# Sobel layers as an interleaved pipeline with 64x64 matmul pairs

## The chip, the core and the metric

The kernel runs on one core of one Trainium2 chip. The metric is the device time of one execution in microseconds (us). A core has five engines that run beside each other, each with its own queue in program order: TensorE (matmuls, PE in the profile, its weight loads PEld), VectorE (DVE), ScalarE (ACT), GpSimd (POOL) and SyncE (SP, which issues transfers). They wait for each other through semaphores. Matmuls write to PSUM, everything else here works on SBUF, both of 128 partitions.

## The reference, cut to what matters

A network of four layers on an image of 256 x 256 pixels with 32 channels. Each layer adds to `x` a function of the group-normalised `x`. Layers 1 and 2, the Sobel layers, are the same: a 3x3 mean, then two Sobel gradients, then their magnitude.

```python
x = x + _L0_conv_ref(_gn(x), ...)     # layernorm, gated projection
x = x + _L1_conv_ref(_gn(x))          # Sobel layer
x = x + _L2_conv_ref(_gn(x))          # Sobel layer
x = x + _L3_conv_ref(_gn(x), ...)     # recurrence over 256 steps

def _L1_conv_ref(x):                  # _L2_conv_ref is the same
    kx, ky = _sobel_kernels(x.shape[-1], x.dtype)
    pooled = _avg_pool3_same(x)       # 3x3 mean, fewer neighbours at the border
    grad_x = _depthwise3(pooled, kx)
    grad_y = _depthwise3(pooled, ky)
    return jnp.sqrt(grad_x * grad_x + grad_y * grad_y + EPSILON)
```

## The kernel before

The image lies in SBUF as `xa` (or `xb`), float32, `[128, 64, 256]`: a block is 4 columns of the image with 32 channels each, which makes the 128 partitions; there are `NB = 64` blocks; the 256 elements of a block run down the image. A Sobel layer reads one of the two images and writes the other.

The filter along the 256 elements is done by additions: `u` adds neighbours, `pp` is the sum of three (with 0 beyond its ends and 1.5 times `u` at them), `v` adds neighbours of `pp`, `sh` neighbours of `v` (smoothing), and `dh` is a difference of `pp`. The filter across image columns is done by matmuls, as it mixes partitions: the block itself and its two neighbours each with a 128x128 matrix from `kt`, three products for each block and gradient. The matrices for the two neighbours (`m` 0 and 2) are zero but for the partitions of the columns next to the block.

```python
NBC = 2                                   # blocks of a step: a pair

def rows_of(ch):
    xs = src[:, ch * NBC : (ch + 1) * NBC, :]
    xn = sp.tile([P, NBC, S], F32, name="xn")
    nc.scalar.activation(xn, xs, AF.Identity, scale=scale, bias=bias)
    u = sp.tile([P, NBC, S - 1], F32, name="u")
    nc.vector.tensor_add(u, xn[:, :, 0 : S - 1], xn[:, :, 1:S])
    pp = sp.tile([P, NBC, S + 2], F32, name="pp")
    nc.gpsimd.memset(pp[:, :, 0 : S + 2 : S + 1], 0.0)
    nc.gpsimd.tensor_scalar(pp[:, :, 1 : S + 1 : S - 1], u[:, :, 0 : S - 1 : S - 2], 1.5, ...)
    nc.vector.tensor_add(pp[:, :, 2:S], u[:, :, 0 : S - 2], xn[:, :, 2:S])
    v = sp.tile([P, NBC, S + 1], F32, name="v")
    nc.vector.tensor_add(v, pp[:, :, 0 : S + 1], pp[:, :, 1 : S + 2])
    sh = kp.tile([P, NBC, S], F32, name="sh")
    nc.gpsimd.tensor_add(sh, v[:, :, 0:S], v[:, :, 1 : S + 1])
    dh = kp.tile([P, NBC, S], F32, name="dh")
    nc.vector.tensor_sub(dh, pp[:, :, 0:S], pp[:, :, 2 : S + 2])
    along[ch] = (sh, dh)

def columns_of(ch):
    ...                                   # pgs: pgx and pgy, [P, 2, S] of PSUM
    for which, pg in enumerate(pgs):
        for b in range(2):
            ...                           # taps: blocks blk - 1, blk, blk + 1
            for i, (n, m) in enumerate(taps):
                nc.tensor.matmul(pg[:, b, :], lhsT=kt[:, k0 + m, :],
                                 rhs=along[n // NBC][which][:, n % NBC, :], ...)
    nc.scalar.activation(sx, pgs[0].rearrange("p b s -> p (b s)"), AF.Square)
    nc.scalar.activation(sy, pgs[1].rearrange("p b s -> p (b s)"), AF.Square)
    nc.gpsimd.tensor_add(ss, sx, sy)
    nc.scalar.activation(mag, ss, AF.Sqrt, bias=sobel_eps)
    nc.vector.tensor_add(d, s, mag)       # residual: d in dst, s in src
    nc.vector.bn_stats(stats[:, blk // 2, :], d)

nch = NB // NBC
rows_of(0)
for ch in range(nch):
    if ch + 1 < nch:
        rows_of(ch + 1)
    columns_of(ch)
return group_norm(stats, ps_n)
```

The order of this code isn't the order in the queues: a scheduler of the framework places the instructions of this part. `xn`, `u`, `pp`, `v`, `sx`, `sy`, `ss` and `mag` have two buffers, `sh` and `dh` five, each of the two PSUM tiles three.

Of the kernel before, what the change touches and what calls it, by code (L numbers as in the profile page):

```python
# [10 lines left out]
F32 = mybir.dt.float32  # L11
AF = mybir.ActivationFunctionType
ALU = mybir.AluOpType
AX = mybir.AxisListType
PSUM = bass.MemoryType.PSUM

S = 256
# [3 lines left out]
NB = T // J  # L21
P = 128
# [9 lines left out]
K_GN, K_CEN, K_AVG, K_SOBEL = 0, 1, 2, 3  # L32
# [26 lines left out]
def net_kernel(  # L59
# [20 lines left out]
    nc = tc.nc  # L80
# [16 lines left out]
    kt = cp.tile([P, NK, P], F32, name="kt")  # L97
    nc.scalar.dma_start(out=kt, in_=consts)

    def eps_tile(value, name):  # L100
        t = cp.tile([P, 1], F32, name=name)
        nc.gpsimd.memset(t, value)
        return t
# [3 lines left out]
    sobel_eps = eps_tile(SOBEL_EPS, "sobel_eps")  # L107
# [24 lines left out]
    NST = NB // 2  # L132

    def new_stats():
        return small.tile([P, NST, nc.vector.BN_STATS_DIM], F32, name="stats")

    def group_norm(stats, psum):

        mv = small.tile([P, nc.vector.BN_AGGR_DIM], F32, name="mv")
        nc.vector.bn_aggr(mv, stats)  # L140
        pm = psum.tile([P, 1], F32, name="pm", tag="pm", bufs=1)
        nc.tensor.matmul(pm, lhsT=kt[:, K_GN, :], rhs=mv[:, 0:1], start=True, stop=True)
        mean = small.tile([P, 1], F32, name="mean")
        nc.vector.tensor_copy(mean, pm)
        d = small.tile([P, 1], F32, name="d")
        nc.vector.tensor_sub(d, mv[:, 0:1], mean)
        q = small.tile([P, 1], F32, name="q")
        nc.vector.scalar_tensor_tensor(q, d, d, mv[:, 1:2], ALU.mult, ALU.add)
        pv = psum.tile([P, 1], F32, name="pv", tag="pm", bufs=1)
        nc.tensor.matmul(pv, lhsT=kt[:, K_GN, :], rhs=q, start=True, stop=True)  # L150
        std = small.tile([P, 1], F32, name="std")
        nc.scalar.activation(std, pv, AF.Sqrt, bias=gn_eps)
        scale = small.tile([P, 1], F32, name="scale")
        nc.vector.reciprocal(scale, std)
        bias = small.tile([P, 1], F32, name="bias")
        nc.vector.scalar_tensor_tensor(bias, mean, -1.0, scale, ALU.mult, ALU.mult)
        return scale, bias


    stats = new_stats()  # L160
    WL = 32
    with tc.tile_pool(name="nat", bufs=3) as natp, tc.tile_pool(
        name="ps_in", bufs=4, space=PSUM
    ) as ps_in:
        for w0 in range(0, T, WL):
# [3 lines left out]
            for b2 in range(WL // (2 * J)):  # L169
# [9 lines left out]
                blk = w0 // J + b2 * 2  # L179
                dst = xa[:, blk : blk + 2, :].rearrange("p b s -> p (b s)")  # L180
# [19 lines left out]
    with tc.tile_pool(name="ln", bufs=3) as lnp, tc.tile_pool(  # L200
        name="ps_ln", bufs=2, space=PSUM
# [7 lines left out]
        for bat in range(NBAT):  # L209
            pvar = ps_var.tile([P, KB, 2, 2, J], F32, name="pvar")  # L210
            for i in range(KB):
                k = bat * KB + i
                src = xa[:, 2 * k : 2 * k + 2, :].rearrange("p b s -> p (b s)")
                dst = xb[:, 2 * k : 2 * k + 2, :].rearrange("p b s -> p (b s)")
                pc = ps_ln.tile([P, 2 * S], F32, name="pc")
                nc.tensor.matmul(pc, lhsT=cen, rhs=src, start=True, stop=True)
                sq = lnp.tile([P, 2, 2, P], F32, name="sq")
# [4 lines left out]
                for b in range(2):  # L222
                    for h in range(2):
                        nc.tensor.matmul(
                            pvar[:, i, b, h, :],
                            lhsT=sq[:, b, h, :],
                            rhs=kt[:, K_AVG, 0:P:C],
                            start=True,
                            stop=True,
# [11 lines left out]
            for i in range(KB):  # L241
                k = bat * KB + i
                pb = ps_ln.tile([P, 2, 2, P], F32, name="pb", bufs=2)
                for b in range(2):
                    for h in range(2):
# [3 lines left out]
                            lhsT=spread[:, r * J : (r + 1) * J, :].rearrange("p j c -> p (j c)"),  # L249
                            rhs=rstdt,  # L250
                            start=True,
                            stop=True,
# [8 lines left out]
    stats = new_stats()  # L261
    with tc.tile_pool(name="at", bufs=3) as atp, tc.tile_pool(
        name="ps_g", bufs=4, space=PSUM
# [55 lines left out]
        gn = group_norm(stats, ps_gn)  # L319


    NBC = 2

    def sobel_layer(src, dst, scale, bias):
        stats = new_stats()
        with tc.tile_pool(name="sob", bufs=2) as sp, tc.tile_pool(
            name="sobk", bufs=5
        ) as kp, tc.tile_pool(name="ps_s", bufs=3, space=PSUM) as ps_s, tc.tile_pool(
            name="ps_n", bufs=1, space=PSUM
        ) as ps_n:  # L330
            along = {}

            def rows_of(ch):

                xs = src[:, ch * NBC : (ch + 1) * NBC, :]
                xn = sp.tile([P, NBC, S], F32, name="xn")
                nc.scalar.activation(xn, xs, AF.Identity, scale=scale, bias=bias)
                u = sp.tile([P, NBC, S - 1], F32, name="u")
                nc.vector.tensor_add(u, xn[:, :, 0 : S - 1], xn[:, :, 1:S])

                pp = sp.tile([P, NBC, S + 2], F32, name="pp")
                nc.gpsimd.memset(pp[:, :, 0 : S + 2 : S + 1], 0.0)  # L342
                nc.gpsimd.tensor_scalar(
                    pp[:, :, 1 : S + 1 : S - 1],
                    u[:, :, 0 : S - 1 : S - 2],
                    1.5,
                    None,
                    ALU.mult,
                )
                nc.vector.tensor_add(pp[:, :, 2:S], u[:, :, 0 : S - 2], xn[:, :, 2:S])  # L350
                v = sp.tile([P, NBC, S + 1], F32, name="v")
                nc.vector.tensor_add(v, pp[:, :, 0 : S + 1], pp[:, :, 1 : S + 2])
                sh = kp.tile([P, NBC, S], F32, name="sh")
                nc.gpsimd.tensor_add(sh, v[:, :, 0:S], v[:, :, 1 : S + 1])
                dh = kp.tile([P, NBC, S], F32, name="dh")
                nc.vector.tensor_sub(dh, pp[:, :, 0:S], pp[:, :, 2 : S + 2])
                along[ch] = (sh, dh)

            def columns_of(ch):
                for b2 in range(NBC // 2):  # L360
                    pgs = [
                        ps_s.tile([P, 2, S], F32, name="pgx"),
                        ps_s.tile([P, 2, S], F32, name="pgy"),
                    ]
                    for which, pg in enumerate(pgs):
                        for b in range(2):
                            blk = ch * NBC + b2 * 2 + b
                            k0 = K_SOBEL + 5 * which
                            mid = 3 if blk == 0 else 4 if blk == NB - 1 else 1
                            taps = [  # L370
                                (n, m)
                                for n, m in ((blk - 1, 0), (blk, mid), (blk + 1, 2))
                                if 0 <= n < NB
                            ]
                            for i, (n, m) in enumerate(taps):
                                nc.tensor.matmul(  # L376
                                    pg[:, b, :],
                                    lhsT=kt[:, k0 + m, :],
                                    rhs=along[n // NBC][which][:, n % NBC, :],
                                    start=(i == 0),  # L380
                                    stop=(i == len(taps) - 1),
                                )
                    blk = ch * NBC + b2 * 2
                    sx = sp.tile([P, 2 * S], F32, name="sx")
                    nc.scalar.activation(sx, pgs[0].rearrange("p b s -> p (b s)"), AF.Square)
                    sy = sp.tile([P, 2 * S], F32, name="sy")
                    nc.scalar.activation(sy, pgs[1].rearrange("p b s -> p (b s)"), AF.Square)  # L387
                    ss = sp.tile([P, 2 * S], F32, name="ss")
                    nc.gpsimd.tensor_add(ss, sx, sy)  # L389
                    mag = sp.tile([P, 2 * S], F32, name="mag")  # L390
                    nc.scalar.activation(mag, ss, AF.Sqrt, bias=sobel_eps)
                    d = dst[:, blk : blk + 2, :].rearrange("p b s -> p (b s)")
                    s = src[:, blk : blk + 2, :].rearrange("p b s -> p (b s)")
                    nc.vector.tensor_add(d, s, mag)
                    nc.vector.bn_stats(stats[:, blk // 2, :], d)

            nch = NB // NBC
            rows_of(0)
            for ch in range(nch):
                if ch + 1 < nch:  # L400
                    rows_of(ch + 1)
                columns_of(ch)
            return group_norm(stats, ps_n)

    gn = sobel_layer(xa, xb, *gn)
    gn = sobel_layer(xb, xa, *gn)
    second.close()

# [379 lines left out]
```

## Time and profile before

| | us |
|---|---|
| median of 3 runs | 3195.89 |
| lowest, highest | 3186.38, 3203.14 |
| profiled execution, span | 3194.4 |
| start of the first Sobel layer's `xn` | 414.8 |
| start of the second one's | 630.5 |
| end of the second, with its statistics | 845.8 |

A profile line of a group or of the order of time names the engine, the line of the kernel, the operation, and the tiles as out<-in; `L389 POOL ... ss<-sx,sy` is GpSimd's sum of the two squares. A float32 matmul of the program shows as two instructions in the trace. In the order of time the first number is the start and the second the length, both in us; what stands in brackets is how long the engine had been idle before, and what ended that. A two-input addition of VectorE that shows more than its usual 0.68 us includes a wait that its queue doesn't show.

The groups of the Sobel layers within the whole of the page: TensorE's `pgx` and `pgy` take 183.3 and 179.4 us for 760 instructions each; the engine was idle 21.6 and 41.2 us just before them.

### The profile page before, as it was taken

How to read it: one execution, taken by the hardware profiler on the slowest of the kernel's cores; microseconds unless marked ns; L12 is line 12 of the kernel's file. 1: busy time of each engine (PE TensorE's matmuls, PEld its weight loads, DVE VectorE, ACT ScalarE, POOL GpSimd, SP SyncE). 2: the span in 40 equal slices, each digit the busy share in tenths (PEclk: the TensorE clock that was granted, in tenths of full speed). 3: DMA queues.
4: the chain of work that ended last, by engine and by line, in shares of the span. 5: the costliest groups of instructions: out<-in, count | busy, mean ns of one | idle time of the engine just before them, and what ended most of it. 6: DMA issues, size and time to landing. Idle time of an engine off the chain costs nothing.

```text
span 3194.4 us, 41235 instructions
## 1 busy us (share of the span) xinstructions
PE 2968.1 (93%) x11221; PEld 1292.2 (40%) x11221; DVE 2708.6 (85%) x6576; ACT 1931.5 (60%) x5272; POOL 1743.4 (55%) x2358
## 2 busy tenths in 40 slices
PE   6999988798799999999999999999999999999998
PEld 4744466576433333333333333333333333333332
DVE  3488886686589999999999999999999999999997
ACT  3255533333266667666666666667666666666665
POOL 0200044454356666666666666666666666666665
PEclk7999999999799999999999999999999999999999
DMA  3000000000000000000000000000000000000000
GB/s 120 1 1 1 1 1 1 1 1 1 26 15 8 14 7 15 15 8 16 8 15 7 14 8 15 15 8 16 8 15 7 14 7 15 15 8 17 2 7 9
DMA packets 29946, 38.56 MB, mean 12 GB/s; under 512 B 6244, under 2 KB 22917, under 8 KB 29704
## 3 DMA queue, kind: packets, MB, share of 16 engines
q1 hardware_dynamic: 27392, 33.57, 3.7%
q10 hardware_dynamic: 2312, 2.25, 0.2%
q8 instruction: 92, 1.51, 0.2%
q14 instruction: 150, 1.23, 0.1%
HBM read 10.63 MB, written 8.39 MB: 6 GB/s over the span
## 4 chain that ended last, share of the span: by engine, by line
DVE 40%; PE 37%; POOL 12%; issue 5%; ACT 4%; DVEq 0%; POOLq 0%; DMA 0%; ACTq 0%
DVE ve L643 13%; PE zz L630 10%; POOL rs L646 9%; DVE zn L650 7%; PE zz L625 7%; DVE c L671 6%; DVE c L679 5%; PE pg L271 3%; PE pt L689 3%; POOL ss L389 2%; PE px L704 2%; PE pv L271 2%; PE zz L614 2%; DVE h L686 2%; PE pg L296 2%
## 5 line engine op out<-in xcount | busy, mean ns | idle before, releaser
L646 POOL TENSOR_TENSOR rs<-ve,mhalf 128x4 f32<-128x4 f32 x1024 | 1035.8, 1012 | 282.5 <-DVE ve L643 240.4
L630 PE MATMUL zz<-wc,hT 128*128 128x512 f32 x2040 | 962.4, 594 | 1.2 <-DVE hT L694 1.2
L666 ACT ACTIVATE ga<-zn 128x384 f32<-128x384 f32 x1024 | 531.2, 519 | 468.0 <-DVE zn L650 467.5
L650 DVE TENSOR_TENSOR zn<-zz,rs 128x512 f32<-128x512 f32 x1024 | 701.3, 685 | 84.0 <-POOL rs L646 76.7
L675 POOL TENSOR_TENSOR fc<-ga,c 128x128 f32<-128x128 f32 x1020 | 464.9, 456 | 523.7 <-ACT ga L666 523.7
L643 DVE TENSOR_REDUCE ve<-sq 128x4 f32<-128x516 f32 x1024 | 697.2, 681 | 16.5 <-POOL sq L581 14.1
L638 ACT ACTIVATE sq<-zz 128x512 f32<-128x512 f32 x1024 | 605.2, 591 | 26.7 <-PE zz L630 13.9
L614 PE MATMUL zz<-fx,xt 33*128 33x512 f32 x2048 | 584.8, 644 | 11.4 <-DVE zn L650 7.6
L625 PE MATMUL zz<-wc,hT 128*128 128x512 f32 x1024 | 525.5, 595 | 0.0
L689 PEld LDWEIGHTS pt<-ident,h 128*128 128x128 f32 x1024 | 142.1, 139 | 805.0 <-DVE h L686 714.3
L630 PEld LDWEIGHTS zz<-wc,hT 128*128 128x128 f32 x2040 | 359.9, 197 | 264.3 <-DVE hT L694 214.1
L683 ACT ACTIVATE th<-c 128x128 f32<-128x128 f32 x1024 | 311.2, 304 | 184.6 <-DVE c L679 179.9
L689 PE MATMUL pt<-ident,h 128*128 128x128 f32 x1024 | 322.1, 315 | 87.6 <-DVE h L686 79.2
L679 DVE TENSOR_TENSOR c<-c,fc 128x128 f32<-128x128 f32 x1020 | 291.4, 286 | 55.4 <-DVE c L671 1.4
L671 DVE TENSOR_TENSOR c<-ga 128x128 f32<-128x128 f32 x1024 | 303.3, 296 | 39.2 <-ACT ga L668 39.2
L668 ACT ACTIVATE ga<-zn 128x128 f32<-128x128 f32 x1024 | 303.1, 296 | 0.0
L686 DVE TENSOR_TENSOR h<-ga,th 128x128 f32<-128x128 f32 x1024 | 291.8, 285 | 0.8 <-ACT th L683 0.8
L614 PEld LDWEIGHTS zz<-fx,xt 33*128 33x128 f32 x2048 | 156.2, 185 | 297.7 <-PE zz L630 226.0
L376 PE MATMUL pgy<-dh,kt 128*128 128x256 f32 x760 | 179.4, 386 | 41.2 <-ACT sy L387 41.2
L342 POOL MEMSET pp<- 128x4 f32 x64 | 6.4, 102 | 379.2 <-PE pg L296 244.7
L376 PE MATMUL pgx<-sh,kt 128*128 128x256 f32 x760 | 183.3, 392 | 21.6 <-POOL pp L342 13.1
L282 ACT ACTIVATE sg<-pg 128x512 f32<-128x512 f32 x256 | 128.9, 627 | 109.6 <-PE pg L271 109.6
(131 smaller groups left out, 2844.0 us busy)
## 6 DMA issues: line engine op xcount, KB each, us to landing
xt<-xa SPq DMA_DIRECT2D x256, 64.0 KB, 2.0
nat<-in_x_dram SPq DMA_DIRECT2D x16, 512.0 KB, 6.5
out_dram<-st SPq DMA_DIRECT2D x32, 256.0 KB, 2.3
wc<-in_L_conv_W_cell_dram ACTq DMA_DIRECT2D x2, 512.0 KB, 4.6
kt<-in_consts_dram ACTq DMA_DIRECT2D x1, 832.0 KB
wv<-in_L_conv_Wv_dram ACTq DMA_DIRECT2D x4, 32.0 KB, 4.5
wg<-in_L_conv_Wg_dram ACTq DMA_DIRECT2D x4, 32.0 KB, 4.2
gamma<-in_L_conv_ln_gamma_dram ACTq DMA_DIRECT2D x4, 0.1 KB, 6.5
```

The source lines that it names most:

```text
L614: nc.tensor.matmul(zz, lhsT=x, rhs=fx[rows, l, :], start=True, stop=l == 0 and t == 0)
L625: nc.tensor.matmul(get("zz"), lhsT=v["hT", 0, t][:, seqs], rhs=wc[:, l, 0, :], start=False, stop=t == 0)
L630: nc.tensor.matmul(get("zz"), lhsT=v["hT", l, t - 1][:, seqs], rhs=wc[:, l, 1, :], start=False, stop=True,)
L638: nc.scalar.activation(sqs[l, h][:, :, 0:H], four(get("zz")), AF.Square, scale=float(H**-0.5))
L643: nc.vector.tensor_reduce(ve, sqs[l, h], AX.X, ALU.add)
L646: nc.gpsimd.tensor_tensor(rs, get("ve"), mhalf, ALU.pow)
L650: nc.vector.tensor_mul(four(zn), four(get("zz")), get("rs").unsqueeze(2).to_broadcast([P, 4, H]))
L666: nc.scalar.activation(ga[:, 0 : 3 * H], get("zn")[:, 0 : 3 * H], AF.Sigmoid)
L671: nc.vector.tensor_mul(c, gates(get("ga"), 0), gates(get("ga"), 3))
L675: nc.gpsimd.tensor_mul(fc, gates(get("ga"), 1), get("c"))
L679: nc.vector.tensor_add(c, c, get("fc"))
L689: nc.tensor.transpose(pt[:, 0:P], get("h"), ident)
```

## The change

The two Sobel layers are written anew; the rest of the kernel stays. Three things change.

First, the order: the instructions of a layer are now placed by a list of times in a period of 4.2 us for each pair of blocks, and the scheduler keeps that order. The parts of one pair are spread over more than three periods, so that each engine works on several pairs in turn.

Second, the matmuls: the product of a block with its own matrix is taken for both blocks of a pair in one matmul of 512 columns (the first and the last pair excepted). The products with the neighbours use only the part of the matrices that isn't zero, a 64x64 corner: for the left neighbour partitions 64 to 127 into 0 to 63, for the right one 0 to 63 into 64 to 127, again for two blocks in one matmul. The two kinds alternate.

Third, the buffers: `sh` and `dh` are rings of 8 blocks, so that two blocks that follow each other lie side by side also across pairs (where the ring ends, the matmul is split in two); `pp` has two fixed buffers, whose zeros are written once for a layer.

```diff
-    NBC = 2
+    RING = 8
+    Q = P // 2
...
+        along = [kp.tile([P, RING, S], F32, name="sh"), kp.tile([P, RING, S], F32, name="dh")]
+        pps = [kp.tile([P, 2, S + 2], F32, name=f"pp{i}") for i in range(2)]
+        for pp in pps:
+            nc.gpsimd.memset(pp[:, :, 0 : S + 2 : S + 1], 0.0)
...
+        def centre(k, which):
+            pg = v["pg", which, k] = ps_s.tile([P, 2, S], F32, name=f"pg{which}")
...
+            if 0 < k < NST - 1:
+                nc.tensor.matmul(
+                    flat(pg),
+                    lhsT=kt[:, k0 + 1, :],
+                    rhs=flat(along[which][:, ring(k), :]),
+                    start=True,
+                    stop=False,
                 )
...
+        def edges(k, which):
...
+            for m, first, rows, cols in (
+                (0, 2 * k - 1, slice(Q, P), slice(0, Q)),
+                (2, 2 * k + 1, slice(0, Q), slice(Q, P)),
+            ):
+                blocks = [(n, n - first) for n in (first, first + 1) if 0 <= n < NB]
+                parts = []
+                if len(blocks) == 2 and (first + 1) % RING:
+                    b = first % RING
+                    parts.append((flat(along[which][rows, b : b + 2, :]), flat(pg[cols])))
+                else:
+                    for n, i in blocks:
+                        parts.append((along[which][rows, n % RING, :], pg[cols, i, :]))
+                sides.append([(kt[rows, k0 + m, cols], rhs, out) for rhs, out in parts])
+            while any(sides):
+                for side in sides:
+                    if side:
+                        w, rhs, out = side.pop(0)
+                        nc.tensor.matmul(out, lhsT=w, rhs=rhs, start=False, stop=not side)
...
+        parts = [
+            (-1.1, normalize, ()),                 # xn
+            (0.0, twos, ()),                       # u
+            (0.6, ends, ()),                       # pp at its ends, GpSimd
+            (0.66, threes, ()),                    # pp
+            (1.32, fours, ()),                     # v
+            (1.98, difference, ()),                # dh
+            (2.05, smooth, ()),                    # sh, GpSimd
+            (2.7, centre, (1,)),
+            (3.56, centre, (0,)),
+            (4.45 + 4.2, edges, (1,)),
+            (5.5 + 4.2, edges, (0,)),
+            (1.4 + 8.4, square, (1,)),
+            (2.5 + 8.4, square, (0,)),
+            (3.5 + 8.4, total, ()),                # ss, GpSimd
+            (0.8 + 12.6, root, ()),                # mag
+            (2.6 + 12.6, residual, ()),
+            (3.25 + 12.6, statistics, ()),         # stats
+        ]
+        todo = [
+            (k * 4.2 + when, k, part, args) for k in range(NST) for when, part, args in parts
+        ]
+        todo.sort(key=lambda e: e[:2])
+        with tc.manual_schedule():
+            for _, k, part, args in todo:
+                part(k, *args)
```

The comments in the list are added here. The parts not shown do what the lines of the same tiles did before, with the same engine for each.

More of the change, by code (lines that the diff above doesn't have):

```diff
@@ L319, in net_kernel, with pair @@
         gn = group_norm(stats, ps_gn)
-    NBC = 2
+    RING = 8
+    Q = P // 2
+    def pair(t, k):
+        return t[:, 2 * k : 2 * k + 2, :].rearrange("p b s -> p (b s)")
     def sobel_layer(src, dst, scale, bias):
         stats = new_stats()
[L326 to L348, printed above, removed]
-                )
[L350 to L402, printed above, removed]
@@ new lines, in sobel_layer @@
+        stack = ExitStack()
+        kp = stack.enter_context(tc.tile_pool(name="sobk", bufs=1))
+        sp = stack.enter_context(tc.tile_pool(name="sob", bufs=2))
+        ps_s = stack.enter_context(tc.tile_pool(name="ps_s", bufs=3, space=PSUM))
+        along = [kp.tile([P, RING, S], F32, name="sh"), kp.tile([P, RING, S], F32, name="dh")]
+        pps = [kp.tile([P, 2, S + 2], F32, name=f"pp{i}") for i in range(2)]
+        for pp in pps:
+            nc.gpsimd.memset(pp[:, :, 0 : S + 2 : S + 1], 0.0)
@@ new lines, in sobel_layer, with flat, ring, normalize @@
+        v = {}
+        def flat(t):
+            return t.rearrange("p b s -> p (b s)")
+        def ring(k):
+            b = 2 * k % RING
+            return slice(b, b + 2)
+        def normalize(k):
+            xn = v["xn", k] = sp.tile([P, 2, S], F32, name="xn")
+            nc.scalar.activation(
+                flat(xn), pair(src, k), AF.Identity, scale=scale, bias=bias
+            )
+        def twos(k):
+            u = v["u", k] = sp.tile([P, 2, S - 1], F32, name="u")
+            xn = v["xn", k]
+            nc.vector.tensor_add(u, xn[:, :, 0 : S - 1], xn[:, :, 1:S])
@@ new lines, in ends, with threes, fours @@
+        def ends(k):
+            nc.gpsimd.tensor_scalar(
+                pps[k % 2][:, :, 1 : S + 1 : S - 1],
+                v["u", k][:, :, 0 : S - 1 : S - 2],
+                1.5,
+                None,
+                ALU.mult,
+            )
+        def threes(k):
+            u, xn = v.pop(("u", k)), v.pop(("xn", k))
+            nc.vector.tensor_add(pps[k % 2][:, :, 2:S], u[:, :, 0 : S - 2], xn[:, :, 2:S])
+        def fours(k):
+            pp = pps[k % 2]
+            w = v["v", k] = sp.tile([P, 2, S + 1], F32, name="v")
+            nc.vector.tensor_add(w, pp[:, :, 0 : S + 1], pp[:, :, 1 : S + 2])
@@ new lines, in smooth, with difference @@
+        def smooth(k):
+            w = v.pop(("v", k))
+            nc.gpsimd.tensor_add(along[0][:, ring(k), :], w[:, :, 0:S], w[:, :, 1 : S + 1])
+        def difference(k):
+            pp = pps[k % 2]
+            nc.vector.tensor_sub(along[1][:, ring(k), :], pp[:, :, 0:S], pp[:, :, 2 : S + 2])
+        def centre(k, which):
+            pg = v["pg", which, k] = ps_s.tile([P, 2, S], F32, name=f"pg{which}")
+            k0 = K_SOBEL + 5 * which
+            b = 2 * k % RING
+            if 0 < k < NST - 1:
[5 more added lines that the diff above has]
+                    stop=False,
+                )
+                return
+            for i in range(2):
+                m = 3 if 2 * k + i == 0 else 4 if 2 * k + i == NB - 1 else 1
+                nc.tensor.matmul(
+                    pg[:, i, :],
+                    lhsT=kt[:, k0 + m, :],
+                    rhs=along[which][:, b + i, :],
+                    start=i == 0,
+                    stop=False,
+                )
@@ new lines, in edges @@
+        def edges(k, which):
+            pg = v["pg", which, k]
+            k0 = K_SOBEL + 5 * which
+            sides = []
+            for m, first, rows, cols in (
[16 more added lines that the diff above has]
+                        nc.tensor.matmul(out, lhsT=w, rhs=rhs, start=False, stop=not side)
@@ new lines, in square, with total, root @@
+        def square(k, which):
+            sq = v["sq", which, k] = sp.tile([P, 2 * S], F32, name=f"sq{which}")
+            nc.scalar.activation(sq, flat(v.pop(("pg", which, k))), AF.Square)
+        def total(k):
+            ss = v["ss", k] = sp.tile([P, 2 * S], F32, name="ss")
+            nc.gpsimd.tensor_add(ss, v.pop(("sq", 0, k)), v.pop(("sq", 1, k)))
+        def root(k):
+            mag = v["mag", k] = sp.tile([P, 2 * S], F32, name="mag")
+            nc.scalar.activation(mag, v.pop(("ss", k)), AF.Sqrt, bias=sobel_eps)
@@ new lines, in residual, with statistics @@
+        def residual(k):
+            nc.vector.tensor_add(pair(dst, k), pair(src, k), v.pop(("mag", k)))
+        def statistics(k):
+            nc.vector.bn_stats(stats[:, k, :], pair(dst, k))
+        parts = [
[17 more added lines that the diff above has]
+        ]
@@ L403, in sobel_layer @@
+        todo = [
[5 more added lines that the diff above has]
+                part(k, *args)
+        stack.close()
+        with tc.tile_pool(name="ps_n", bufs=1, space=PSUM) as ps_n:
             return group_norm(stats, ps_n)
```

## The prediction

> **What bounds the kernel now.** I read the page's slices first, then the busy time by stage, then the order of time inside one Sobel stage. The slices only say that something between slices 5 and 10 uses VectorE less than its surroundings; the table by stage says how much time is at stake. Its columns are the stretch, its length, busy us and instruction count of TensorE matmuls, TensorE weight loads, VectorE, ScalarE and GpSimd, then the granted clock, DMA share and GB/s.
>
> ```profile
> 414.80:630.50 215.70, 178.35 (x764) 144.01 (x764) 154.28 (x199) 80.10 (x130) 104.72 (x128) 0.97 0.00 1
> 630.50:845.80 215.30, 178.01 (x764) 143.79 (x764) 155.59 (x199) 80.12 (x129) 105.55 (x132) 0.97 0.01 5
> 880.00:3194.00 2314.00, 2216.53 (x7412) 790.55 (x7412) 2107.23 (x5692) 1590.55 (x4671) 1496.73 (x2044) 0.99 0.04 11
> ```
>
> The two Sobel layers are the first two lines: 215.7 + 215.3 = 431.0 us, 13.5% of 3194.4. The recurrence, the third line, is 2314 us and isn't touched. So the change can only move those 431 us, and 2% of the whole (64 us) is 15% of them. No engine is full there: TensorE shows 83%, VectorE 72%.
>
> Next the order of time in the middle of the first Sobel layer (start, duration, engine, line, what):
>
> ```profile
> 522.43 1.64 POOL L389 TENSOR_TENSOR ss<-sx,sy 128x512 f32<-128x512 f32 x1 [0.64 <-ACT sy L387]
> 524.10 0.72 ACT L391 ACTIVATE mag<-ss,sobel_eps 128x512 f32<-128x512 f32 x1 [1.81 <-POOL ss L389]
> 524.86 0.69 DVE L394 TENSOR_TENSOR xb<-xa,mag 128x512 f32<-128x512 f32 x1 [1.91 <-ACT mag L391]
> 525.59 0.69 DVE L395 BATCH_NORM_STATS2 stats<-xb 128x6 f32<-128x512 f32 x1
> 526.20 0.68 DVE L356 TENSOR_TENSOR dh<-pp 128x512 f32<-128x512 f32 x1
> 527.13 0.69 DVE L350 TENSOR_TENSOR pp<-u,xn 128x508 f32<-128x508 f32 x1 [0.26 <-POOL pp L342]
> 527.92 1.34 DVE L352 TENSOR_TENSOR v<-pp 128x514 f32<-128x514 f32 x1
> 529.19 0.68 DVE L339 TENSOR_TENSOR u<-xn 128x510 f32<-128x510 f32 x1
> 529.35 1.65 POOL L389 TENSOR_TENSOR ss<-sx,sy 128x512 f32<-128x512 f32 x1 [0.64 <-ACT sy L387]
> ```
>
> From one ss to the next: 529.35 - 522.43 = 6.92 us for a pair of blocks (16 pairs in the 110 us from 480 to 590 give 6.88). The lines form a ring: ss lets mag go, mag lets the residual xb go, VectorE then works off stats, dh, pp, v, u in its fixed order, which lets ScalarE make xn, then sy, then the next ss. Each engine waits for the latest result of another one. The bound is this ring of waits, not an engine.
>
> But one thing in it isn't a wait of the program: v takes 1.34 us and not 0.69, ss 1.64. The reason shows best at the start of the layer, where VectorE only makes rows:
>
> ```profile
> 420.36 0.68 DVE L339 TENSOR_TENSOR u<-xn 128x510 f32<-128x510 f32 x1
> 420.96 0.68 DVE L352 TENSOR_TENSOR v<-pp 128x514 f32<-128x514 f32 x1
> 421.57 0.68 DVE L356 TENSOR_TENSOR dh<-pp 128x512 f32<-128x512 f32 x1
> 421.73 1.42 POOL L354 TENSOR_TENSOR sh<-v 128x512 f32<-128x512 f32 x1
> 422.17 1.52 DVE L350 TENSOR_TENSOR pp<-u,xn 128x508 f32<-128x508 f32 x1
> 423.61 0.68 DVE L339 TENSOR_TENSOR u<-xn 128x510 f32<-128x510 f32 x1
> 428.67 1.52 DVE L350 TENSOR_TENSOR pp<-u,xn 128x508 f32<-128x508 f32 x1
> 429.61 1.71 POOL L389 TENSOR_TENSOR ss<-sx,sy 128x512 f32<-128x512 f32 x1
> 430.11 1.75 DVE L339 TENSOR_TENSOR u<-xn 128x510 f32<-128x510 f32 x1
> 613.87 1.27 POOL L389 TENSOR_TENSOR ss<-sx,sy 128x512 f32<-128x512 f32 x1 [1.87 <-ACT sy L387]
> ```
>
> VectorE's two-input operations follow each other at 0.60 us (420.36, 420.96, 421.57). Then sh waits for dh to finish reading, and pp waits for sh: pp runs 1.52, 0.84 more than 0.68. A ss costs the next VectorE addition 1.75 - 0.68 = 1.07. Where only stats was at work beside it (the last line, at the end of the layer, where no rows are left to make), ss took 1.27 and stats, a line I don't repeat, its usual 0.69: one-input operations aren't held. So GpSimd's sh and ss and VectorE's additions take turns: 0.84 and 1.07 us of VectorE's time per pair.
>
> **What the Trainium skill says.** "SBUF — State Buffer", Who interferes with whom: a VectorE instruction with two SBUF inputs contends with a GpSimd instruction that reads SBUF, and the second to come blocks until the first is done. The trace agrees, with the 0.84 and 1.07 above. "TensorE: Matmul & The Clock Gate", Part 3, Packing small matmuls: matmuls on different row or column tiles run at the same time. The trace agrees for four column tiles and for four row tiles in the attention layer:
>
> ```profile
> 228.53 1.92 PE L296 MATMUL pg<-o,wo 128*32 128x512 f32 x16
> ```
>
> 16 instructions of 512 columns in 1.92 us, of which one alone is 0.59; one after the other, at the 0.43 us each that two of the Sobel layer's 256-column ones take (12 in 2.59 us where they are dense, from 612.30 to 614.89: 0.216 each), they would take 6.9. "TensorEngine Tiling (Array Packing)" has two warnings: Key Properties, a change of tiling mode drains the array; and Gotcha 1, row tiles can't access the same PSUM bank at once. The changed kernel's two 64x64 tiles differ in rows and columns but write halves of the same bank. No line of the trace before shows that case.
>
> **The change part by part, per pair of blocks.** The new program order on VectorE is u, pp, v, dh, then the residual and stats of three pairs earlier; on GpSimd ends, sh, then ss of two pairs earlier; on ScalarE mag, two squares, xn; on TensorE two centre products and the edge products of the pair before. All results that cross engines are now made about a period earlier than they are used, so the ring of waits goes away, and the fullest resource sets the period.
>
> TensorE, removed: 24 instructions x 0.216 = 5.2 us. Added: centre 2 x 2 instructions x 0.43 = 1.72; edges, if each diagonal pair runs side by side, another 1.72; drains, two mode changes at some 0.17 (0.59 for one instruction minus 0.43 of streaming, my estimate): 0.3. Sum 3.8. No longer near the bound.
>
> ScalarE: 0.81 + 0.58 + 0.58 + 0.72 = 2.7. Unchanged, not the bound. The memset of pp, 0.10 on GpSimd, leaves the loop, and with it the 0.26 that pp waited for.
>
> VectorE with the shared turns: starts in a row are 0.60 apart; where an operation needs the result just before it the step is longer, 0.75 from u to pp and 0.79 from pp to v (527.13 to 527.92), 0.72 from the residual to stats (524.86 to 525.59). So u 0.75, pp 0.79, v 0.60, dh 0.60, residual 0.72, stats 0.61: 4.07. That is the 4.2 period for which the new order is laid out. On top come the turns. sh becomes ready when v ends, while dh reads; it goes in after dh and holds the residual for 0.84. ss is next on GpSimd, gets in when the residual has read (0.60 after its start), and holds 1.07, to 1.67. Meanwhile stats runs unhindered; the next u would have started at 0.72 + 0.61 = 1.33, and starts at 1.67: ss costs only 0.34. ends hides beside pp. Period: 4.07 + 0.84 + 0.34 = 5.25, against 6.9.
>
> The layer: first xn 0.9; three opening periods without residual or ss, 0.75 + 0.79 + 0.60 + 0.60 + 0.84 = 3.6 each, 10.8; 28 full periods, 147.0; the last pair from its u to its stats: v done at 2.2, dh at 2.9, centres to 4.6, four edge groups of 1.05 to 8.8 (0.86 plus drain), square 9.6, ss 11.0, mag 11.8, residual and stats 13.2; then statistics to the next layer's first xn, 3.8 as now (626.7 to 630.5). Sum 175.7, against 215.5 on average. Twice the difference of 39.8 is 80 us; I keep 4 us back for hand-overs of the turn, some of which showed 0.1 us more. 3195.9 - 76 = 3120 us.
>
> **The rivals.** (A) The turns cost nothing because the new order happens to place GpSimd's work beside stats only: period 4.2, saving 28 x 1.05 x 2 = 59 us more, 3061. Against it: sh falls due exactly beside dh and the residual, and 1.04 + 1.27 us of GpSimd don't fit beside one 0.6 us stats. (B) The 64x64 pairs don't run side by side, for the shared bank: edges 3.44, TensorE 5.2 + 0.3 = 5.5 becomes the bound, 28 x 0.25 x 2 = 14 us, and 4 x 0.86 = 3.4 in each layer's last pair, 7 us: 3141. For it speaks Gotcha 1; against it in part the L296 line, whose four column tiles share a bank, though all of them use the same rows. (C) ss doesn't fall beside stats but holds up an addition in full: 1.07 in place of 0.34, 28 x 0.73 x 2 = 41 us: 3161. (D) TensorE, now idle a third of each period, gets a lower clock. At half clock, 1.0 to 0.5, it would need 2 x 3.44 + 0.3 = 7.2 us a pair, the layer would take 0.9 + 31 x 7.2 + 15 + 3.8 = 243 us, and the kernel 55 us more than now. Against it: idle stretches are below 2 us each, and between 480 and 590 the clock was 1.00 with waits of over 1 us in each period.
>
> **Range and chances.** Centre 3120; A in part would give 3085, C in full or B with some of C 3165. 2% of 3195.9 is 64 us, so faster needs less than 3132; the centre is 12 us inside, B and C are outside. Faster 0.62, same 0.34, slower 0.04 (D or a wait that I overlooked).
>
> **What would show it right or wrong.** Right: ss to ss 5.2 to 5.4 us in mid-layer; about 176 us a layer; the VectorE operation behind sh (the residual) at some 1.5 us, u slightly lengthened, stats at 0.69; the diagonal pair of two 512-column products within about 1.05 us; TensorE waiting for VectorE and GpSimd rather than for ScalarE. Wrong: a period of 4.2 with short additions (A), edge groups of 1.9 us and VectorE idle behind TensorE (B), u at 1.7 us (C), a granted clock under 0.9 in the stage (D), or any change of the 2314 us of the recurrence.

## The result and the profile after

| | us |
|---|---|
| before, median of 4 runs beside the change | 3191.22 |
| changed, median of 4 runs | 3108.03 (3103.57 to 3120.22) |
| ratio | 0.974, 95% interval 0.970 to 0.978 |

The change is 2.6% faster, 83 us by the medians; 3120 was predicted. I read the profile after in the same order as the one before. First the busy time by stage, with the columns of before:

```profile
400.70:579.30 178.60, 125.14 (x452) 46.72 (x452) 162.82 (x198) 81.39 (x129) 116.14 (x98) 0.96 0.00 1
579.30:757.50 178.20, 124.83 (x452) 46.46 (x452) 162.70 (x198) 81.40 (x129) 117.75 (x102) 0.96 0.02 6
792.00:3104.00 2312.00, 2216.71 (x7412) 790.23 (x7412) 2106.47 (x5691) 1592.47 (x4671) 1498.89 (x2044) 0.99 0.04 11
```

The Sobel layers went from 215.7 and 215.3 us to 178.6 and 178.2: 74.2 us. The recurrence stands where it stood, 2312 against 2314 us. TensorE's busy time fell from 178 to 125 us a layer; VectorE's rose from 154 to 163, though it does the same work: it now contains more waits for its turn, which a busy time doesn't show apart.

Of the 90 us between the two profiled spans another 14 lie ahead of the Sobel layers, in code that both kernels share. They come from the clock that TensorE was granted in the layernorm stage, which differs from one execution to the next (last section), so from here on I compare layers and periods, not only totals.

Now the order of time in mid-layer, VectorE and GpSimd with three of TensorE's groups, two of edges and one of a centre:

```profile
524.00 1.07 PE L434 MATMUL pg<-dh,kt 64*64 64x512 f32 x4
524.06 1.03 DVE L361 TENSOR_TENSOR u<-xn 128x510 f32<-128x510 f32 x1
524.91 1.02 PE L434 MATMUL pg<-sh,kt 64*64 64x512 f32 x4
525.12 0.69 DVE L374 TENSOR_TENSOR pp<-u,xn 128x508 f32<-128x508 f32 x1
525.93 0.69 DVE L379 TENSOR_TENSOR v<-pp 128x514 f32<-128x514 f32 x1
526.54 0.69 DVE L387 TENSOR_TENSOR dh<-pp 128x512 f32<-128x512 f32 x1
526.77 1.35 POOL L383 TENSOR_TENSOR sh<-v 128x512 f32<-128x512 f32 x1 [0.88 <-ACT sq L438]
527.14 1.53 DVE L449 TENSOR_TENSOR xb<-xa,mag 128x512 f32<-128x512 f32 x1
527.37 1.10 PE L394 MATMUL pg<-dh,kt 128*128 128x512 f32 x2 [1.43 <-ACT xn L354]
528.09 1.71 POOL L442 TENSOR_TENSOR ss<-sq,sq 128x512 f32<-128x512 f32 x1
528.71 0.69 DVE L452 BATCH_NORM_STATS2 stats<-xb 128x6 f32<-128x512 f32 x1
529.32 1.03 DVE L361 TENSOR_TENSOR u<-xn 128x510 f32<-128x510 f32 x1
```

From u to u 5.26 us; over 28 pairs the mean is 5.254. No VectorE line has idle time ahead of it: the queue is full. The residual (xb) takes 1.53 because sh has the turn, u 1.03 in place of 0.69 because the end of ss is still in its way, and stats its usual 0.69 in the middle of ss. Four 64x64 instructions of 512 columns take 0.91 us from group to group (524.00 to 524.91), not four times 0.43: the two diagonal tiles run side by side.

### The profile page after: what moved, and what is told of

Read it like the earlier page. It is cut to its first block, busy times and chain, and to the rows that moved or that the text cites. A ratio compares the mean times of both kernels' runs of the same rounds, so it can differ in the third digit from the quotient of the medians.

```text
span 3104.5 us, 40153 instructions
## 1 busy us (share of the span) xinstructions
PE 2847.4 (92%) x10597; PEld 1088.2 (35%) x10597; DVE 2723.7 (88%) x6576; ACT 1936.5 (62%) x5272; POOL 1769.9 (57%) x2298
## 3 DMA queue, kind: packets, MB, share of 16 engines
q10 hardware_dynamic: 2312, 2.25, 0.2%
## 4 chain that ended last, share of the span: by engine, by line
DVE 44%; PE 38%; POOL 10%; issue 4%; ACT 2%; DVEq 0%; POOLq 0%; DMA 0%; ACTq 0%
DVE ve L722 13%; PE zz L709 10%; POOL rs L725 9%; DVE zn L729 7%; PE zz L704 7%; DVE c L750 6%; DVE c L758 5%; PE pg L271 4%; PE pt L768 4%; PE px L783 2%; PE pv L271 2%; PE zz L693 2%; PE pg L296 2%; DVE h L765 2%; DVE u L361 2%
## 5 line engine op out<-in xcount | busy, mean ns | idle before, releaser
L709 PEld LDWEIGHTS zz<-wc,hT 128*128 128x128 f32 x2040 | 359.6, 196 | 264.7 <-DVE hT L773 213.6
L704 PEld LDWEIGHTS zz<-wc,hT 128*128 128x128 f32 x1024 | 183.3, 219 | 2.3 <-issue 2.3
L290 DVE TENSOR_TENSOR o<-pv,sg 128x512 f32<-128x512 f32 x256 | 156.0, 680 | 22.4 <-PE pv L271 19.1
L773 DVE COPY hT<-pt 128x128 f32<-128x128 f32 x512 | 142.9, 279 | 9.7 <-PE pt L768 3.2
```

The source lines that it names most:

```text
L704: nc.tensor.matmul(get("zz"), lhsT=v["hT", 0, t][:, seqs], rhs=wc[:, l, 0, :], start=False, stop=t == 0)
L709: nc.tensor.matmul(get("zz"), lhsT=v["hT", l, t - 1][:, seqs], rhs=wc[:, l, 1, :], start=False, stop=True,)
```

## The experiments

**One: is it the order or the matmuls?** The two halves of the change, each alone. First the new order with the old matmuls:

```diff
 def edges(k, which):        # and every matmul 256 columns wide
-    64x64 pairs, two blocks wide
+    for each block and each neighbour: whole 128x128 matrix kt[:, k0 + m, :]
```

> The new order and rings, but the neighbours' products with the whole 128x128 matrices, and every matmul 256 columns as before. My theory (order first; VectorE's steps and the turns with GpSimd set the period): TensorE needs 24 x 0.216 = 5.2 us a pair, just under the 5.25 of the turns, so the period stays at 5.25 to 5.4 and the time between 3108 and 3120 us. Rival (the smaller matmuls bring the gain): TensorE near its limit can't follow, period 5.6 or more, time 3135 us or more.

Measured 3115.36 us, ratio to before 0.979 (0.975 to 0.983); period 5.26, layer 181.1. My theory held: with TensorE filled to 5.2 of 5.26 us the period is the same, and the layer is 2.4 us longer, nearly all of it at its two ends. The smaller matmuls are not needed for the gain.

Then the new matmuls with the calls in the old sequence, placed by the scheduler:

```diff
-        parts = [(-1.1, normalize, ()), ...]
-        with tc.manual_schedule(): ...
+        rows_of(0)
+        for k in range(NST):
+            if k + 1 < NST:
+                rows_of(k + 1)      # normalize, twos, ends, threes, fours, smooth, difference
+            columns_of(k)           # centre, edges, square, total, root, residual, statistics
```

> The rings, wide centre matmuls and 64x64 pairs, but the instructions of a pair called in the order of the kernel before and placed by the framework's scheduler, as there. My theory: the ring of waits (ss, mag, residual, stats, dh, pp, v, u, xn, square) stays; only TensorE's part gets shorter, and TensorE wasn't in the ring for long. Period 6 to 6.9 us, time 3150 to 3190 us: most of the gain is missing. Rival (the matmuls bring it): period near 5.25 and 3110 to 3120 us.

My theory fell here: 3124.93 us, ratio 0.980 (0.977 to 0.983), and a layer of 177.6 us, as short as the changed kernel's. So neither half is needed if the other is there. Both kernels keep the third part of the change, the rings and the two fixed `pp` buffers; what these bring alone, with the old matmuls and the scheduler's order, no run here shows. The order of time shows why this isn't the old order at all:

```profile
503.40 0.68 DVE L379 TENSOR_TENSOR v<-pp 128x514 f32<-128x514 f32 x1
503.70 1.06 ACT L438 ACTIVATE sq<-pg 128x512 f32<-128x512 f32 x2
504.00 0.68 DVE L449 TENSOR_TENSOR xb<-xa,mag 128x512 f32<-128x512 f32 x1
504.61 1.52 DVE L387 TENSOR_TENSOR dh<-pp 128x512 f32<-128x512 f32 x1
505.55 1.71 POOL L442 TENSOR_TENSOR ss<-sq,sq 128x512 f32<-128x512 f32 x1
506.06 0.68 DVE L452 BATCH_NORM_STATS2 stats<-xb 128x6 f32<-128x512 f32 x1
506.66 1.15 DVE L374 TENSOR_TENSOR pp<-u,xn 128x508 f32<-128x508 f32 x1
507.72 0.68 DVE L361 TENSOR_TENSOR u<-xn 128x510 f32<-128x510 f32 x1
508.32 0.68 DVE L379 TENSOR_TENSOR v<-pp 128x514 f32<-128x514 f32 x1
```

The scheduler, given other instructions and buffers, placed them differently: both squares run together, not with xn between them, and VectorE is full, with its turns. Here u lies between pp and v, so neither waits for the result just before it: v to v is 4.92 us (other stretches of this layer run at 5.2 to 5.5). What had made the old order slow was therefore more particular than "results are used too soon"; the third set looks for it.

**Two: are the turns between VectorE and GpSimd the bound?** First the step of the prediction that hides most of ss beside stats, undone by moving stats alone:

```diff
-            (3.25 + 12.6, statistics, ()),     # after the residual, before u
+            (0.3 + 16.8, statistics, ()),      # after u, before pp
```

> One instruction moved: stats is placed between u and pp of a later pair, in place of between the residual and u. My theory: ss on GpSimd then has no VectorE operation beside it that doesn't take turns, and holds u up in full; steps 0.61 + 0.61 + 0.79 + 0.60 + 0.60 + 0.84 + 1.67 = 5.72 us a period, 0.47 more, and about 3134 us; u shows some 1.7 us. Rival (the period comes from a ring through ScalarE and TensorE, or from the sum of VectorE's busy time): no change, 5.25 and 3108 us.

3135.22 us, ratio 0.985 (0.981 to 0.990); period 5.71, layer 191.7, against 5.72 and 3134 expected.

```profile
501.20 1.71 POOL L442 TENSOR_TENSOR ss<-sq,sq 128x512 f32<-128x512 f32 x1
501.71 1.75 DVE L361 TENSOR_TENSOR u<-xn 128x510 f32<-128x510 f32 x1
503.38 0.68 DVE L452 BATCH_NORM_STATS2 stats<-xb 128x6 f32<-128x512 f32 x1
```

u stands behind ss for the full 1.06 us, with stats too late to fill the time. The same instructions on the same engines, one in another place: 13 us a layer (191.7 against 178.6).

Then a pair that differs in one operand. ss goes from GpSimd to VectorE, which is the fuller engine, and everything that doesn't take turns is put beside sh. In one kernel a square lies in PSUM, in the other both are in SBUF:

```diff
-            nc.gpsimd.tensor_add(ss, v.pop(("sq", 0, k)), v.pop(("sq", 1, k)))
+            nc.vector.tensor_add(ss, v.pop(("sq", 0, k)), v.pop(("sq", 1, k)))
...
+        ps_q = stack.enter_context(tc.tile_pool(name="ps_q", bufs=2, space=PSUM))
+            pool = sp if which else ps_q       # ss_vector_psum alone
...
+            (3.0 + 4.2, edges, (1,)), (4.0 + 4.2, edges, (0,)),
+            (2.45 + 8.4, square, (0,)), (2.5 + 8.4, total, ()), (4.0 + 8.4, root, ()),
+            (0.3 + 12.6, residual, ()), (2.55 + 12.6, statistics, ()),
```

> ss moves from GpSimd to VectorE, one of its two squares is put in PSUM, and it and stats follow dh; the residual goes between u and pp; edges of dh go ahead of the centre product of sh. VectorE has one instruction more. My theory: ss and stats each read SBUF once at most, so that sh runs beside them without a turn; seven steps of 0.60, one of them 0.79: period 4.4 to 4.6, some 156 to 162 us a layer, 3063 to 3075 us. Rival (VectorE is full and only the number of its operations counts): 5.25 + 0.6 = 5.85, 3144 us.

> As ss_vector_psum with the same instructions on the same engines in the same order, but both squares in SBUF. My theory: sh now makes ss wait for 0.84, so the period is 4.4 + 0.84 = 5.25 and the time about 3108 us, some 40 us above ss_vector_psum, and ss shows 1.5 us. Rival (number of operations counts): the same time as ss_vector_psum, whatever that is.

With both squares in SBUF: 3111.37 us, ratio 0.978 (0.973 to 0.982), period 5.24, layer 177.8. With one in PSUM: 3098.1 us, ratio 0.972 (0.969 to 0.976), mean period 4.74, layer 164.0; both the time and the period are above what I expected. The order of time at the same place, SBUF first, then PSUM:

```profile
504.75 1.35 POOL L383 TENSOR_TENSOR sh<-v 128x512 f32<-128x512 f32 x1 [1.46 <-DVE v L379]
505.12 1.53 DVE L442 TENSOR_TENSOR ss<-sq,sq 128x512 f32<-128x512 f32 x1
506.57 0.68 DVE L452 BATCH_NORM_STATS2 stats<-xb 128x6 f32<-128x512 f32 x1
```

```profile
505.19 1.35 POOL L384 TENSOR_TENSOR sh<-v 128x512 f32<-128x512 f32 x1 [1.46 <-DVE v L380]
505.41 0.58 ACT L440 ACTIVATE sq<-pg 128x512 f32<-128x512 f32 x1 [1.40 <-PE pg L435]
506.02 0.69 DVE L444 TENSOR_TENSOR ss<-sq,sq 128x512 f32<-128x512 f32 x1 [0.38 <-ACT sq L440]
```

ss takes 1.53 against 0.69 us: 0.84, to the hundredth what sh cost before. The same seven operations take 5.24 us with both squares in SBUF and 4.74 with one in PSUM, so the number of operations isn't the bound; who may read SBUF at that moment is. The missed part is 4.74 against the 4.4 to 4.6 expected: the last line shows ss waiting 0.38 for a square. The next kernel moves stats ahead of ss and restores TensorE's order:

```diff
-            (3.0 + 4.2, edges, (1,)), (4.0 + 4.2, edges, (0,)), ... (2.55 + 12.6, statistics, ()),
+            (4.45 + 4.2, edges, (1,)), (5.5 + 4.2, edges, (0,)), ... (2.0 + 12.6, statistics, ()),
```

> ss_vector_psum had a period of 4.74, not 4.4 to 4.6: ss waited up to 0.4 us for the square of sh's gradient. Here stats goes ahead of ss, and TensorE has the changed kernel's order again (both centres, then the edges), which has two changes of tile shape a pair and not four. If that wait is all that was missing: period 4.4 to 4.5, some 156 to 159 us a layer, 3062 to 3070 us. If TensorE itself is the bound in that kernel (four matmul groups in 4.15 us with their gaps): 4.6 or more, no faster than 3078 us.

> The changed kernel once more, on the same chip as the two others, for the comparison: 5.25 us a period, 178 us a layer.

3087.3 us, ratio 0.970 (0.968 to 0.973), layer 162.2; the changed kernel in the same set 3110.93 us, ratio 0.976 (0.975 to 0.978), layer 178.4. It is the fastest version here, 16 to 17 us less in each of the two layers than the changed kernel. But the period is 4.68. The time and the period are those that I had written for TensorE as the bound, and yet TensorE isn't the bound: in each period it waits 0.86 us for dh (first line), while VectorE shows what is missing:

```profile
502.89 1.10 PE L395 MATMUL pg<-dh,kt 128*128 128x512 f32 x2 [0.86 <-DVE dh L388]
503.26 0.68 DVE L444 TENSOR_TENSOR ss<-sq,sq 128x512 f32<-128x512 f32 x1
503.85 0.68 DVE L362 TENSOR_TENSOR u<-xn 128x510 f32<-128x510 f32 x1
503.97 0.72 ACT L448 ACTIVATE mag<-ss,sobel_eps 128x512 f32<-128x512 f32 x1 [0.60 <-DVE ss L444]
504.73 0.70 DVE L451 TENSOR_TENSOR xb<-xa,mag 128x512 f32<-128x512 f32 x1 [0.19 <-ACT mag L448]
```

ss no longer waits, but now it comes so late that the residual, two places on, waits for its mag: 0.88 from u to xb in place of 0.60. That is the missing 0.28.

**Three: what made the old order slow?** I wrote the Sobel layer before as a list in exactly the order that its scheduler had given each engine in mid-layer (nothing else changed), as a control, and then edited single places:

> The kernel before, its Sobel layer written out as a list in the order that the scheduler had given each engine in mid-layer (VectorE: xb, stats, dh, pp, v, u; ScalarE: mag, sx, xn, sy; GpSimd: ss, memset, ends, sh). Nothing else changes. It is the control of the next three: period 6.8 to 6.9 us, 3180 to 3195 us.

Period 6.92, as in the kernel before. The time, 3213.57 us, ratio 1.005 (1.003 to 1.007), is above what I expected: a layer takes 223.4 us and not 215.7, because its opening is longer in the list (the fifth ss comes 52.9 us after the first xn, against 45.4). The next runs are therefore best compared by their periods.

```diff
-                (sx, 1), (xn, 9), (sy, 1),        # ScalarE
+                (sx, 1), (sy, 1), (xn, 9),
```

> As before_listed, with two neighbours on ScalarE swapped: sy ahead of xn. In the ring of waits, sy (and so ss) stands behind xn, which waits for pp to free a buffer that nobody needs for a long time. My theory: the ring is two rings; this opens the one through xn and leaves the one through the memset (ss, mag, xb, stats, dh, memset, ends, sh, ss), which is 0.6 us shorter: period 6.2 to 6.4. Rival (the many matmuls held up the old order): no change, 6.9.

Period 6.32, 3182.64 us, ratio 0.995 (0.993 to 0.997): the period is as expected.

```diff
-                v["pp", k] = sp.tile([P, NBC, S + 2], F32, name="pp")
-                nc.gpsimd.memset(t("pp", k)[:, :, 0 : S + 2 : S + 1], 0.0)
+                v["pp", k] = pps[k % 2]           # zeros written once
```

> As before_listed, with two fixed buffers for pp whose zeros are written once: no memset in the loop. My theory: GpSimd's queue no longer waits for dh, but the ring through xn stays, less the 0.26 us between dh and pp: period 6.6 to 6.7. Rival (the memset alone was the old order's trouble): 5.2 to 5.5.

Missed: period 6.32, 3170.3 us, ratio 0.993 (0.991 to 0.995). That is 0.60 less a period where I had counted 0.26: the wait between dh and pp is gone, as expected, and u now comes after ss has got its turn, so that ss takes 1.27 us and not 1.65.

> Both edits: sy ahead of xn and no memset in the loop. Old matmuls, old order on VectorE. My theory: both rings are open, and VectorE's six steps with the two turns are left: period 5.2 to 5.8, 3115 to 3150 us; nearly the whole gain of the change without its matmuls and without its order. Rival (the gain needs fewer matmuls or operations a period or more ahead of their use): 6.2 or more.

Missed: 6.29, 3181.35 us, ratio 0.994 (0.992 to 0.997), as the rival had it. Two edits, and the same period as with either. The order of time of before_both says what is left:

```profile
526.23 1.71 POOL L425 TENSOR_TENSOR ss<-sx,sy 128x512 f32<-128x512 f32 x1
527.98 0.72 ACT L429 ACTIVATE mag<-ss,sobel_eps 128x512 f32<-128x512 f32 x1 [1.89 <-POOL ss L425]
528.73 0.69 DVE L435 TENSOR_TENSOR xb<-xa,mag 128x512 f32<-128x512 f32 x1 [0.24 <-ACT mag L429]
529.46 0.70 DVE L438 BATCH_NORM_STATS2 stats<-xb 128x6 f32<-128x512 f32 x1
530.07 0.68 DVE L381 TENSOR_TENSOR dh<-pp 128x512 f32<-128x512 f32 x1
530.91 0.65 POOL L354 TENSOR_SCALAR pp<-u 128x4 f32<-128x4 f32 x1 [2.96 <-DVE dh L381]
531.52 1.03 POOL L375 TENSOR_TENSOR sh<-v 128x512 f32<-128x512 f32 x1
532.52 1.72 POOL L425 TENSOR_TENSOR ss<-sx,sy 128x512 f32<-128x512 f32 x1
```

Read the bracket of the sixth line: GpSimd is idle 2.96 us until dh has run. It wasn't the memset that waited but whatever writes the pp buffer next; now that is ends, four elements a partition, and sh and ss queue behind it. The data that they need has been there for long. The remedy is a third buffer:

```diff
-            pps = [kp.tile([P, NBC, S + 2], F32, name=f"pp{i}", bufs=1) for i in range(2)]
+            pps = [kp.tile([P, NBC, S + 2], F32, name=f"pp{i}", bufs=1) for i in range(3)]
```

> before_both stayed at 6.29 us. Its trace shows why: without the memset, ends waits for the same thing, dh, which has to have read the pp buffer that ends writes next; and ends stands ahead of sh and ss in GpSimd's queue. Here pp has three fixed buffers in place of two, nothing else changes. My theory: ends then waits for the dh of a period earlier, the ring through GpSimd opens, and with the one through xn open already the turns are left: period 5.2 to 5.8 us, 3115 to 3150 us, with the old matmuls and VectorE's old order. Rival (the old order needs fewer matmuls or operations spread over periods): 6.0 or more.

Period 5.36, 3129.39 us, ratio 0.981 (0.976 to 0.986), layer 184.0: the old matmuls and VectorE's old sequence, and most of the gain (a layer of 223.4 us in the control, 178.6 in the changed kernel). The page's table of waits for this kernel, from 480 to 560 us (who waited for what, us in total, times, longest), shows the ring through GpSimd gone:

```profile
ACT xn L336 <- DVE pp L363: 38.5, 13, 3.0
POOL sh L375 <- DVE v L369: 14.5, 16, 1.5
POOL pp L354 <- DVE dh L381: 8.9, 14, 0.6
```

ends still waits for dh, but 0.6 us and not 3.0. The xn that waits 3.0 us holds up little: u follows v by 0.83 us in place of 0.60, because it starts only when xn has ended.

```profile
520.56 0.81 ACT L336 ACTIVATE xn<-xa,bias,scale 128x512 f32<-128x512 f32 x1 [2.96 <-DVE pp L363]
520.57 0.69 DVE L369 TENSOR_TENSOR v<-pp 128x514 f32<-128x514 f32 x1
521.40 0.69 DVE L342 TENSOR_TENSOR u<-xn 128x510 f32<-128x510 f32 x1
```

## Why the prediction was right, and where it was not

- **The bound before, a ring of waits: right, and now shown.** It was two rings that share ss, mag, residual, stats and dh: one back through pp, xn and sy, which the prediction named, and one through pp's buffer, ends and sh, which it didn't see. Both hang on places in in-order queues. Opening the first alone gives 6.32, opening both 5.36; opening the second alone, with a third buffer and the old order of sy and xn, was not run.
- **The period of the changed kernel: right, in its terms too.** 5.25 predicted, 5.254 measured; the residual shows the 0.84 for sh (1.53 against 0.69), u the 0.34 for ss (1.03 against 0.69). The runs with stats moved (5.71 against 5.72) and with one square in PSUM (ss 0.69 against 1.53) confirm the terms singly.
- **Rivals.** A (turns cost nothing) is out, by the residual at 1.53. B (64x64 tiles one after the other) is out, by 0.91 us a group; the warning about a shared PSUM bank that the prediction cites for it doesn't hold for these two tiles, which differ in rows and columns. C didn't come in the changed kernel (u 1.03); the run with stats moved shows what it would have looked like (u 1.75). D didn't come: 1.00 of the clock in mid-layer, 0.96 over the layer.
- **The removal of matmul time.** The prediction had TensorE at 3.8 us a pair (from the starts, 0.95 + 0.93 + 0.91 and the last group are some 3.7) and said that it is no longer near the bound. True, but the old 5.2 us would have done as well; the first experiment shows that with the new order this term was worth 2.4 us a layer, nearly all at its ends. For most of the waits of TensorE's centre products the profile names ScalarE's xn, where the prediction expected VectorE and GpSimd. No matmul reads xn, and in the lines of the profile after the product starts 0.14 us after its dh has ended (527.37 against 527.23), so dh is the likelier cause; that isn't shown.
- **Mis-sized terms.** The layer took 178.6 us against a sum of 175.7. As in the sum, a period is counted here from where u has got its turn (its end less 0.69 us), not from where its line starts. Opening: 12.5 us against 10.8, because the third opening period is 5.3, with u waiting 2.0 us for an xn that stands behind two squares. Last pair: 14.25 against 13.2. The 28 full periods are 147.1 against 147.0, the statistics 3.9 against 3.8. The 4 us that I kept back covered most of this: 74.2 us in the layers, 76 predicted. The 83 us between the medians are no better confirmation: the 9 us beyond the layers lie outside what was changed, where the layernorm stage alone moves an execution by 15, and that the total fell 12 us below 3120 is chance as far as these runs show.
- **What I had not seen:** that the order as a whole isn't needed. "Made about a period earlier than they are used" is sufficient, not necessary; in the listed old order, a swap of two instructions and three fixed `pp` buffers do nearly the same.

## What to carry to other kernels

When every engine of a loop waits for another one, follow the queues and not the data: an instruction that needs a free buffer, or has data to wait for, holds up all behind it, and one more buffer or one swap opens the ring. Once the queue is full, count what takes turns: a VectorE operation with two SBUF inputs and GpSimd's reads exclude each other (0.84 and 1.07 us a turn here), so put one-input operations, or ones with an operand in PSUM, beside GpSimd's (0.69 us each, no wait). A faster engine off the bound brings little, even if it is the busiest in the profile: in the new order, the smaller matmuls were worth 2.4 us a layer. And where a scheduler places the instructions, look at the order that came out: with the new matmuls and buffers it found, unasked, one as good as the written list.

## What the runs showed of the hardware

An operation more on the fuller engine was a gain: with one square in PSUM, VectorE's seven operations and GpSimd's sh took 4.74 us a pair, with both in SBUF 5.24, and six operations with GpSimd's sh and ss 5.25.

In the layernorm stage, which all kernels here share, the granted TensorE clock from 50 to 100 us was 0.58 to 0.60 in some executions and 0.93 to 0.96 in others, with no difference in the program before that time; the columns are those of the stages above, for the kernel before and then the changed one:

```profile
50.00:100.00 50.00, 48.23 (x180) 34.76 (x181) 14.31 (x23) 11.36 (x18) 3.05 (x4) 0.59 0.00 1
```

```profile
50.00:100.00 50.00, 47.63 (x287) 36.38 (x288) 23.49 (x37) 16.34 (x26) 7.50 (x10) 0.93 0.00 1
```

TensorE is busy 48 of the 50 us in both, and does 180 instructions against 287, as 0.59 is to 0.93. In the profiles with the lower clock the first Sobel layer starts at 414 to 416 us, in those with the higher one at 397 to 401. The changed kernel's own two profiles are one of each, with 0.93 and 0.58: they start it at 400.7 and 416.0, 15 us apart, while the layer takes 178.6 and 178.4. What decides it, no run here shows. A total that differs by half a per cent says little before the stages have been compared.
